# Row gathers of the third and fourth tile issued behind the first packed-query gathers

## The chip, the cores and the metric

The kernel runs on one core of a Trainium2 chip. The time is the device time of one execution in microseconds (us). The numbers for a kernel are the median, the lowest and the highest of several executions; beside them stands one execution taken with the hardware profiler, from which all durations, waits and start times in this text come. Times "at 692.27" are us from the start of the profiled span.

The engines have short names in the profile: PE multiplies matrices, PEld is its weight load, DVE is the vector engine, ACT the scalar engine, POOL the GpSimd engine, SP the engine that issues most plain DMAs. POOL issues the indirect DMAs (row gathers through a list of indices) beside its own arithmetic.

## The reference

Four graph layers run one after the other on x of 8 batches x 2048 nodes x 64 channels. Every layer normalises its input, attends over the neighbours of each node that a sparse 2048 x 2048 matrix names, and adds the result to x.

```python
# --- layer 0 (adj_preln) ---
h = jnp.maximum(_layernorm(x, axis=-1), 0.0)
x = x + _L0_gnn_ref(h, adj)
# --- layer 1 (adj_preln) ---
h = jnp.maximum(_layernorm(x, axis=-1), 0.0)
x = x + _L1_gnn_ref(h, adj, L1_gnn_W, L1_gnn_a)
# --- layer 2 (adj_preln) ---
h = jnp.maximum(_layernorm(x, axis=-1), 0.0)
x = x + _L2_gnn_ref(h, adj, L2_gnn_Wh, L2_gnn_bh, L2_gnn_Wo, L2_gnn_bo, L2_gnn_gamma, L2_gnn_beta)
# --- layer 3 (adj_preln) ---
h = jnp.maximum(_layernorm(x, axis=-1), 0.0)
x = x + _L3_gnn_ref(h, adj, L3_gnn_W, L3_gnn_a)
```

The change lies in layer 2, in its first half, which has four heads (H = 4, D = 64):

```python
def _gat_layer(h, mask, b):
    scores = jnp.einsum('...nd,...md->...nm', h, h)
    scores = jnp.where(mask, scores, NEG)
    attn = jax.nn.softmax(scores, axis=-1)
    return jnp.einsum('...nm,...md->...nd', attn, h) + b
...
h = jnp.einsum('bnc,hdc->bhnd', x, Wh)
out_h = _gat_layer(h, mask[None, None], bh[None, :, None, :])
cat = jnp.transpose(out_h, (0, 2, 1, 3)).reshape(B, N, H * D)
z = jax.nn.leaky_relu(cat, negative_slope=0.2)
h2 = jnp.einsum('bnk,dk->bnd', z, Wo)
out2 = _gat_layer(h2, mask[None], bo)
```

Since q·k of two projected nodes is x_n (Wh^T Wh) x_m, the kernel stores per node the products x_n (Wh^T Wh) of all heads once, and then scores each edge against the plain row x_m of the neighbour.

## The kernel before

**Tiles and slots.** The 2048 nodes are cut into 16 tiles of 128. In a tile, each of the 128 nodes sits on one partition. The first neighbours of each node fill whole slots: `ROWS[i]` slots of tile i hold one neighbour for every node. The further neighbours of the nodes that have more are packed: `PACKED[i]` slots of tile i hold an arbitrary edge on each partition. A slot's neighbour rows come by one indirect DMA, "a row gather", which POOL issues in `gather` (L246 to L255): 128 rows of 512 numbers of 4 bytes, 256 KB, into one of the 26 places of `ring` (`RING`, L33), a buffer that all tiles share in turn. A tile's places come free when its last user is done.

**The queries of the four heads.** At the end of layer 1 `products` (L321 to L336) makes for each tile the 2080 numbers per node (8 batches x 4 heads x 64, and 32 norms) and SP stores them in the table `qtab` (L336), 1040 KB per tile. For a `ROWS` slot the tile's own products `q` serve as they are: for the first two tiles of layer 2 they are still in SBUF (`kept`), for the others SP loads them (L741) into one of two buffers. For a packed slot each partition needs the products of another node, so POOL gathers them from `qtab` (L730, `qe`, 1040 KB each) into one of `QE` = 4 buffers. `fetch` issues those gathers in the order of use; the fifth needs the buffer of the first, which is free once DVE has subtracted the norms (L760) of the first.

**Layer 2, first half** (L714 to L850). `pipeline(take2, first2, second2, third2, fourth2)` runs the tiles in the order `ORDER2 = [8, 9, 10, 12, 11, 13, 0, ...]`, each stage one tile behind the stage ahead of it:
- `take2` issues the row gathers of the tile, the load of its own rows (L736), the load of `q` (L741) and up to four `qe` gathers.
- `first2` scores: per slot ACT copies the row to PSUM (`g2`, L753, one buffer), DVE multiplies it with `q` or `qe` (L755), sums (L759), subtracts (L760), and ACT takes the exponential (`w`, L761).
- `second2` weights: per slot and per pair of heads k POOL multiplies row and weight (`wh`, L772, three buffers) and for some tiles adds two such products (L785); PE sums them over slots in PSUM (L787), starting from the tile's own rows (L779); ACT divides (`yn`, L795).
- `third2` and `fourth2` project with PE, ACT and DVE and store the rows that the second attention reads.

Slots of the first tiles, `ROWS` + `PACKED`: tile 8 has 3 + 1, tile 9 has 3 + 1, tile 10 has 3 + 1, tile 12 has 1 + 2, tile 11 has 1 + 2, tile 13 has 2 + 1, tile 0 has 9 + 8. The first six sum to 21 slots; the ring of 26 has room for five of tile 0.

**What sets the order.** The text of the program doesn't fix the order on an engine. The Tile framework takes the instructions with their dependencies and lays out each engine's sequence itself, with a simulated timeline (`schedule_with_timeline_sim=True`). On the chip each engine then runs its sequence as laid out, and waits where a semaphore isn't there yet. In the sequence before, POOL issues around the start of layer 2's first half: 26 row gathers, four `qe` gathers, three L772 and one L785 of tile 8, a fifth `qe` gather, and then L772 of tile 8's packed slot. Each DMA of POOL signals on one of eight semaphores in turn, and waits, before it is issued, for the DMA eight before it.

Of the kernel before, what the change touches and what calls it, by code (L numbers as in the profile page):

```python
# [1 line left out]

# [32 lines left out]

PAIRS = [0, 0, 2, 2, 2, 0, 0, 0, 2, 2, 2, 2, 2, 2, 2, 2]
QE = 4


MAKING = [15, 14, 13, 0, 12, 11, 10, 1, 9, 2, 8, 3, 7, 4, 6, 5]  # L40
# [19 lines left out]
def edge_stack(ctx: ExitStack, tc: tile.TileContext, x_in, adj, w1, w1t, a1, wh, wht, bh, wo, bo,  # L60
# [9 lines left out]
    nc = tc.nc  # L70
# [141 lines left out]
    order = list(MAKING)  # L212
# [33 lines left out]
    def gather(k, i, st):  # L246

        n = SLOTS[i]
        assert sum(SLOTS[j] for j in held) + n <= RING
        held[i], front[0] = front[0], (front[0] + n) % RING  # L250
        cols = table[k].shape[1]
        for t in range(n):
            nc.gpsimd.indirect_dma_start(  # L253
                out=ring[:, (held[i] + t) % RING, :cols], out_offset=None, in_=table[k][:, :],
                in_offset=bass.IndirectOffsetOnAxis(ap=idx[:, OFF[i] + t:OFF[i] + t + 1], axis=0))  # L255

    def load(st, name, src, bufs):
        st[name] = rows_pool[0].tile([P, F], F32, name=name, bufs=bufs)
        nc.sync.dma_start(out=st[name], in_=src)

    def rows_of(k, i):
        return table[k][i * P:(i + 1) * P, :F]
# [451 lines left out]
    with tc.tile_pool(name="l2", bufs=2) as l2p, \  # L714
# [5 lines left out]
        thin[0] = ps_z  # L720

        stream = [(i, t) for i in order for t in range(PACKED[i])]
        sent = {}

        def fetch(upto):

            while len(sent) <= min(upto, len(stream) - 1):
                i, t = stream[len(sent)]
                q = sent[i, t] = l2p.tile([P, QW], F32, name="qe", bufs=QE)
                nc.gpsimd.indirect_dma_start(  # L730
                    out=q, out_offset=None, in_=qtab[:, :],
                    in_offset=bass.IndirectOffsetOnAxis(ap=qidx[:, POFF[i] + t:POFF[i] + t + 1], axis=0))

        def take2(i, st):
            gather(2, i, st)
            load(st, "rows", rows_of(2, i), 3)  # L736
            if i in order[:2]:
                st["q"] = kept[i]
            else:
                st["q"] = own_pool[0].tile([P, QW], F32, name="q")  # L740
                nc.sync.dma_start(out=st["q"], in_=qtab[i * P:(i + 1) * P, :])  # L741
            fetch(stream.index((i, 0)) + min(PACKED[i], QE) - 1)

        def score(i, st, lo, hi):

            K, n = ROWS[i], hi - lo
            w = l2p.tile([P, max(ROWS), B * H], F32, name="w2", bufs=5)[:, :n]
            st.setdefault("w", []).append(w)
            s = ps_s.tile([P, F], F32, name="s2")[:, :n * B * H].rearrange("p (t c) -> p t c", c=B * H)
            for t in range(lo, hi):  # L750
                q = st["q"] if t < K else sent[i, t - K]
                g = ps_g.tile([P, F], F32, name="g2")
                nc.scalar.copy(g, row(i, t))  # L753
                pr = l2p.tile([P, B * H, D], F32, name="prod2")
                nc.vector.tensor_tensor(  # L755
                    pr.rearrange("p (b h) d -> p b h d", h=H),
                    q[:, :B * H * D].rearrange("p (b h d) -> p b h d", h=H, d=D),
                    heads(g)[:, :, None, :].to_broadcast([P, B, H, D]), op=OP.mult)
                nc.vector.tensor_reduce(s[:, t - lo, :], pr, AX.X, OP.add)  # L759
                nc.vector.tensor_tensor(s[:, t - lo, :], s[:, t - lo, :], q[:, B * H * D:], op=OP.subtract)  # L760
                nc.scalar.activation(w[:, t - lo], s[:, t - lo], AF.Exp, bias=mbb[:, OFF[i] + t:OFF[i] + t + 1])  # L761
                if t >= K:
                    fetch(stream.index((i, t - K)) + QE)

# [66 lines left out]
        def fourth2(i, st):  # L831
# [14 lines left out]
            store_rows(3, i, h2, False)  # L846

        pipeline(take2, first2, second2, third2, fourth2)
        thin[0] = None
    own.close()  # L850
# [541 lines left out]
def whole_stack(tc, t, out):  # L1392
    nc = tc.nc
    D = t["gamma"].shape[0]
    with tc.tile_pool(name="flag", bufs=1) as pool:
        flag = pool.tile([1, 1], I32, name="flag")
        edge_stack(tc, t["x"], t["adj"], t["w1"], t["w1t"], t["a1"], t["wh"], t["wht"], t["bh"], t["wo"],
                   t["bo"], t["gamma"], t["beta"], t["w3"], t["w3t"], t["a3"], out, flag)
        bad = nc.values_load(flag, min_val=0, max_val=1)
        with tc.If(bad > 0):  # L1400
            gnn_stack(tc, t["x"].rearrange("n (b d) -> n b d", d=D), t["adj"], t["w1"], t["a1"], t["wht"],
                      t["bh"], t["wo"], t["bo"], t["gamma"], t["beta"], t["w3"], t["a3"],
                      out.rearrange("n (b d) -> n b d", d=D))
# [36 lines left out]
```

## Time and profile before

| what | value |
|---|---|
| three executions | median 1720.55 us, 1719.27 to 1725.79 us |
| the profiled execution, device time | 1721.51 us |
| its span from first to last instruction | 1719.7 us |
| mean granted PE clock in it | 0.875 |
| busy in the span: PE, DVE, POOL, ACT | 1215.1, 1318.4, 1153.4, 744.5 us |
| row gathers (L253), all layers | 405, 986 ns each on POOL |
| `qe` gathers (L730) | 32, 986 ns each on POOL |
| L772 `wh` | 162, 1918 ns each on POOL |
| L755 and L759, the two long DVE steps of one scored slot | 2276 to 2282 ns and 2286 ns |

The first half of layer 2 lies between about 660 and 1215 us of the span. In the groups of instructions, "busy" is the sum over a group, "idle before" the time in which the engine stood still just ahead of the group's members, with what ended most of it. A DMA issued by POOL shows there only the time of its issue; when its data have landed shows in who waited for it. In the timeline a bracket gives the idle time before an instruction and what ended it. "issue" means that nothing in the profile was waited for.

### The profile page before, as it was taken

The numbers are of one execution on the slowest core, as the hardware profiler recorded it, in microseconds if no ns is written. First come the engines' busy times: TensorE is split into PE (matmuls) and PEld (weight loads), VectorE is DVE, ScalarE is ACT, GpSimd is POOL, SyncE is SP. The second block draws the span as 40 slices with busy tenths as digits, with TensorE's granted clock in tenths as the row PEclk, the third lists the DMA queues.
The fourth block names the chain that finished last, engine by engine and source line by source line (L and its number), as shares of the span: only waits on it lengthen the run. The fifth ranks groups of instructions, "written<-read, shape, count | busy, mean of one in ns | idle before, by whom it ended". The sixth has DMA issues, their size and how long they took to land.

```text
span 1719.7 us, 15784 instructions
## 1 busy us (share of the span) xinstructions
PE 1215.1 (71%) x3771; PEld 606.6 (35%) x3771; DVE 1318.4 (77%) x2748; ACT 744.5 (43%) x2378; POOL 1153.4 (67%) x903
## 2 busy tenths in 40 slices
PE   0025667776479974599997999999467877555877
PEld 0002334443234431234342444443223433333545
DVE  6979999992469987699997899831389889823656
ACT  5841324441146783356531545545234445620011
POOL 5766867786554125898789889985577896654540
PEclk9998876896699997799999999999787879657989
DMA  5555454455566447656255345200643542235651
GB/s 172 167 182 179 152 200 153 141 198 156 147 201 235 158 179 260 233 189 208 87 201 200 113 157 177 87 13 19 255 141 99 154 146 70 81 119 164 197 170 51
DMA packets 85787, 266.94 MB, mean 155 GB/s; under 512 B 14627, under 2 KB 14659, under 8 KB 75446
## 3 DMA queue, kind: packets, MB, share of 16 engines
q0 software_dynamic: 37328, 141.05, 26.7%
q1 hardware_dynamic: 48358, 124.79, 20.4%
q8 instruction: 32, 0.52, 0.1%
q14 instruction: 69, 0.57, 0.1%
HBM read 208.74 MB, written 57.05 MB: 155 GB/s over the span
## 4 chain that ended last, share of the span: by engine, by line
PE 25%; POOL 11%; DVE 9%; issue 7%; ACT 5%; DMA 3%; another core or an unknown queue 2%; DVEq 0%; SPq 0%; POOLq 0%; ACTq 0%
PE y L787 10%; PE y L385 4%; POOL g L253 3%; POOL wh L772 3%; PE m L836 2%; ACT yn L795 2%; PE m L824 2%; PE y L779 2%; POOL wg L380 1%; DMA g<-table,idx 1%; POOL ln_r L290 1%; DMA rows<-table 1%; PE m L399 1%; DVE prod L755 1%
## 5 line engine op out<-in xcount | busy, mean ns | idle before, releaser
L253 POOL DMA_INDIRECT g<-table,idx x405 | 399.2, 986 | 233.5 <-issue 161.7
L772 POOL TENSOR_TENSOR wh<-g,w 128x1024 f32<-128x1024 f32 x162 | 307.5, 1918 | 30.0 <-PE y L787 28.0
L385 PE MATMUL y<-wg,ident 128*128 128x512 f32 x392 | 234.5, 729 | 72.7 <-POOL wg L380 64.3
L290 POOL TENSOR_TENSOR ln_r<-ln_q,mhalf 128x8 f32<-128x8 f32 x80 | 135.8, 1701 | 160.6 <-DVE ln_q L288 85.1
L759 DVE TENSOR_REDUCE s<-prod 128x32 f32<-128x2048 f32 x81 | 184.0, 2286 | 14.8 <-ACT w L761 12.9
L380 POOL TENSOR_TENSOR wg<-g,w 128x1024 f32<-128x1024 f32 (+1 forms) x91 | 158.9, 1756 | 37.3 <-ACT w L436 24.2
L787 PE MATMUL y<-wh,ident 128*128 128x512 f32 x320 | 154.6, 610 | 28.9 <-POOL wh L785 25.1
L385 PE MATMUL y<-wg,selt 128*128 128x512 f32 x256 | 141.6, 663 | 5.4 <-POOL wg L380 4.4
L385 PEld LDWEIGHTS y<-wg,ident 128*128 128x128 f32 x392 | 81.6, 228 | 162.2 <-POOL wg L380 78.9
L787 PE MATMUL y<-wh,selt 128*128 128x512 f32 x256 | 124.7, 614 | 10.4 <-POOL wh L772 10.4
L795 ACT ACTIVATE yn<-y,rec 128x64 f32<-128x64 f32 x512 | 111.2, 368 | 27.5 <-PE y L787 26.9
L755 DVE TENSOR_TENSOR prod<-q,g 128x2048 f32<-128x2048 f32 x49 | 111.5, 2276 | 5.3 <-ACT g L753 4.6
L399 PE MATMUL m<-w,selt 128*128 128x8 f32 (+1 forms) x384 | 59.5, 258 | 76.0 <-ACT w L542 38.2
L380 DVE TENSOR_TENSOR wg<-g,tiny 128x1024 f32<-128x1024 f32 (+1 forms) x92 | 98.2, 1086 | 17.1 <-PE y L385 8.8
L399 PEld LDWEIGHTS m<-w,selt 128*128 128x128 f32 x384 | 63.5, 213 | 122.3 <-ACT w L542 43.6
L442 DVE SCALAR_TENSOR_TENSOR zt<-m,bhc,att 128x512 f32<-128x512 f32 x64 | 47.3, 738 | 75.0 <-ACT att L441 74.4
L298 ACT ACTIVATE xh<-x,ln_r 128x64 f32<-128x64 f32 x256 | 88.3, 428 | 18.8 <-POOL ln_r L292 18.7
L787 PEld LDWEIGHTS y<-wh,ident 128*128 128x128 f32 x320 | 59.0, 193 | 104.9 <-issue 63.8
L428 PE MATMUL q<-rows,sel 128*128 128x512 f32 x128 | 84.3, 762 | 15.7 <-DVE prod L422 5.0
L753 ACT COPY g<-g 128x512 f32<-128x512 f32 x81 | 50.4, 622 | 100.5 <-DVE prod L755 87.9
L755 DVE TENSOR_TENSOR prod<-qe,g 128x2048 f32<-128x2048 f32 x32 | 73.0, 2282 | 17.0 <-DMA qe<-qtab,qidx 15.9
L779 PE MATMUL y<-rows,ident 128*128 128x512 f32 x128 | 70.0, 634 | 18.3 <-DMA rows<-table 13.6
(210 smaller groups left out, 2584.7 us busy)
## 6 DMA issues: line engine op xcount, KB each, us to landing
qtab<-q SPq DMA_DIRECT2D x16, 1040.0 KB
a<-in_adj_dram SPq DMA_DIRECT2D x16, 1024.0 KB
q<-qtab SPq DMA_DIRECT2D x14, 1040.0 KB
table<-xh SPq DMA_DIRECT2D x48, 256.0 KB
rows<-table SPq DMA_DIRECT2D x48, 256.0 KB
xs<-x SPq DMA_DIRECT2D x48, 256.0 KB
x<-xs SPq DMA_DIRECT2D x48, 256.0 KB
table<-xh SPq DMA_DIRECT2D x32, 260.0 KB
```

The lines of the kernel that those rows point to most:

```text
L253: nc.gpsimd.indirect_dma_start(out=ring[:, (held[i] + t) % RING, :cols], out_offset=None, in_=table[k][:, :], in_offset=bass.IndirectOffse ...
L290: nc.gpsimd.tensor_tensor(st["rstd"][:, 0, :], q, mhalf, op=OP.pow)
L298: nc.scalar.activation(dst[:, b * D:(b + 1) * D], st["src"][:, b * D:(b + 1) * D], func, bias=0.0 if st["less"] is None else r[:, 1, b:b + ...
L380: eng.tensor_tensor(wg[:, :m].rearrange("p t (b d) -> p t b d", b=B), g[:, :, :F].rearrange("p t (b d) -> p t b d", b=B), w[:, t0:t0 + m, ...
L385: nc.tensor.matmul(y, lhs(i, t), wg[:, t - t0, :], start=(t == 0 and own is None), stop=(t == n - 1))
L399: nc.tensor.matmul(p[:, :cols], selt(i, t), packed[:, t, :], start=(t == 0), stop=(t == T - 1))
L755: nc.vector.tensor_tensor(pr.rearrange("p (b h) d -> p b h d", h=H), q[:, :B * H * D].rearrange("p (b h d) -> p b h d", h=H, d=D), heads(g ...
L759: nc.vector.tensor_reduce(s[:, t - lo, :], pr, AX.X, OP.add)
L772: nc.gpsimd.tensor_tensor(wg, heads(row(i, t))[:, :, None, :].to_broadcast([P, B, 2, D]), w[:, :, 2 * k:2 * k + 2, None].to_broadcast([P, ...
L779: nc.tensor.matmul(st["ys"][j], ident, xb[:, 4 * j:4 * j + 4], start=True, stop=False)
L787: nc.tensor.matmul(st["ys"][j], lhs(i, t), wg[:, 4 * j:4 * j + 4], start=False, stop=(t == n - 1))
L795: nc.scalar.activation(yn[:, b, h, :], st["ys"][j][:, b, h, :], AF.Copy, scale=st["rec"][:, 4 * j + b, 2 * k + h:2 * k + h + 1])
```

## The change

In `take2` the row gathers of the tiles at places 2 and 3 of the order (the third and the fourth, tiles 10 and 12) get an edge to a `qe` gather: the one that was newest when `take2` of the tile two places ahead had ended. For tile 10 that is the `qe` gather of tile 8, for tile 12 that of tile 9. `issue_after` adds no wait on a semaphore: it tells the scheduler that each of these seven gathers has to stand behind that instruction in POOL's sequence. Nothing is added or removed; every gather moves the same bytes to the same place.

```diff
+BEHIND, LATER = 2, 4
...
-        sent = {}
+        sent, newest, lately = {}, [None], []
...
                 q = sent[i, t] = l2p.tile([P, QW], F32, name="qe", bufs=QE)
-                nc.gpsimd.indirect_dma_start(
+                newest[0] = nc.gpsimd.indirect_dma_start(
                     out=q, out_offset=None, in_=qtab[:, :],
                     in_offset=bass.IndirectOffsetOnAxis(ap=qidx[:, POFF[i] + t:POFF[i] + t + 1], axis=0))
 
         def take2(i, st):
-            gather(2, i, st)
+
+            n = order.index(i)
+            with tc.issue_after(lately[n - BEHIND].ins) if BEHIND <= n < LATER else nullcontext():
+                gather(2, i, st)
             load(st, "rows", rows_of(2, i), 3)
...
             fetch(stream.index((i, 0)) + min(PACKED[i], QE) - 1)
+            lately.append(newest[0])
```

The sequences that the scheduler lays out differ as follows. POOL, from the start of layer 2's first half, before: 26 row gathers; `qe` 1 to 4; L772 x3 and L785 of tile 8; `qe` 5; L772 of tile 8's packed slot. After: 19 row gathers; `qe` 1 to 4; 4 row gathers; L772 x3 and L785 of tile 8; `qe` 5; 3 row gathers; L772 of tile 8's packed slot. From there the two sequences hold the same instructions, with `qe` gathers shifted by one to four places among the L772, forward for the next tiles and backward within tile 0.

On ACT, up to tile 0, copies of rows and exponentials of the scores (L753, L761) stand ahead of eight-fold groups of divisions (L795) behind which they stood before, at seven places; the long DVE steps move ahead of short ones in the same way. On SP, five loads and stores move by up to two places. From the middle of tile 0's packed slots the sequences agree again for the rest of layer 2's first half.

The second half of layer 2 and layer 3's start (L859 to L902, between about 1255 and 1530 us of the span) touch nothing that the change touches, but the scheduler lays them out anew: there 330 DVE instructions, 297 of ACT, 170 of PE and 60 of POOL stand at other places than before, by at most 18, 25, 12 and 5 places. The largest moves belong to two tiles whose divisions and layer norms (L465, L881 to L883, L890) go 15 to 18 places back and forward. Layer 3's rest is as before.

More of the change, by code (lines that the diff above doesn't have):

```diff
@@ L1 @@
-from contextlib import ExitStack
+from contextlib import ExitStack, nullcontext
 import concourse.bass as bass
```

## The prediction

> **What bounds the kernel now.** I looked first at where in the span the change lies, with the busy time of each engine by stretch (columns: stretch, its length; busy time and instructions of PE, PEld, DVE, ACT, POOL; PE clock; share of the DMA engines' time; GB/s).
>
> ```profile
> 660.00:684.60 24.60, 7.20 (x12) 2.16 (x10) 22.17 (x18) 5.70 (x12) 18.66 (x20) 0.63 0.90 319
> 684.60:701.00 16.40, 0.00 (x0) 0.00 (x0) 0.52 (x2) 0.00 (x0) 13.48 (x13) 0.50 0.91 314
> 701.00:770.00 69.00, 59.28 (x154) 23.91 (x154) 67.59 (x59) 36.16 (x121) 63.57 (x39) 0.93 0.55 186
> 770.00:806.70 36.70, 35.95 (x106) 16.38 (x105) 33.97 (x33) 22.21 (x77) 34.08 (x24) 1.00 0.69 231
> 806.70:828.50 21.80, 18.82 (x58) 8.13 (x58) 20.56 (x19) 15.21 (x50) 15.91 (x10) 1.00 0.24 78
> 828.50:890.60 62.10, 59.75 (x181) 26.87 (x179) 60.63 (x47) 27.53 (x75) 46.49 (x30) 1.00 0.48 163
> 890.60:950.50 59.90, 44.48 (x102) 18.25 (x102) 47.40 (x43) 17.55 (x57) 55.65 (x40) 0.94 0.56 186
> 950.50:1100.00 149.50, 148.68 (x429) 66.75 (x430) 138.14 (x116) 78.45 (x247) 132.44 (x83) 1.00 0.45 149
> ```
>
> From 684.6 to 701 PE and ACT do nothing and DVE nearly nothing: only POOL and the DMA engines work. That hole is what the change can shorten. From 701 on three engines are almost full at once, so a shorter hole need not be a shorter program; PE is fullest from 770 to 890 and from 950 on, POOL between. Then the timeline of the hole (start, length, engine, instruction; in brackets the idle time before it and what ended it):
>
> ```profile
> 684.24 0.32 SPq L741 DMA_DIRECT2D q<-qtab  x1
> 684.25 0.29 ACT L761 ACTIVATE w<-s,mbb 128x32 f32<-128x32 f32 x1 [2.60 <-issue]
> 684.57 0.26 DVE L403 TENSOR_REDUCE row<-w 128x32 f32<-128x96 f32 x1 [0.35 <-issue]
> 684.75 0.95 POOL L253 DMA_INDIRECT g<-table,idx  x1 [0.31 <-issue]
> ...
> 691.02 0.95 POOL L253 DMA_INDIRECT g<-table,idx  x1 [0.30 <-issue]
> 692.27 0.95 POOL L730 DMA_INDIRECT qe<-qtab,qidx  x1 [0.31 <-issue]
> ...
> 696.98 5.65 POOL L772 TENSOR_TENSOR wh<-g,w 128x1024 f32<-128x1024 f32 x3
> 700.71 2.29 DVE L755 TENSOR_TENSOR prod<-qe,g 128x2048 f32<-128x2048 f32 x1 [15.88 <-DMA qe<-qtab,qidx]
> 702.58 2.34 POOL L785 TENSOR_TENSOR wh<-wh 128x1024 f32<-128x1024 f32 x1
> ...
> 704.98 6.60 PE L787 MATMUL y<-wh,ident 128*128 128x512 f32 x8 [22.20 <-POOL wh L785]
> ...
> 707.90 0.98 POOL L730 DMA_INDIRECT qe<-qtab,qidx  x1 [2.97 <-DVE s L760]
> 708.90 5.65 POOL L772 TENSOR_TENSOR wh<-g,w 128x1024 f32<-128x1024 f32 x3
> ```
>
> DVE had scored tile 8's three plain slots by 684.6 and waited 15.88 us for the first `qe`. POOL issued it only at 692.27, behind 26 row gathers at one per 1.255 us from 659.58. PE waited 22.2 us for the first L785: the weights of tile 8 were there at 684.5 (the exponential at 684.25), but POOL's multiplications stood behind the last seven row gathers and four `qe` issues. Last, could `qe` have gone earlier? SP's own waits:
>
> ```profile
> SPq L741 <- DMA qtab<-q: 3.7, 1, 3.7
> SPq L741 <- DVE s L760: 7.4, 2, 6.9
> ```
>
> The load of `q` stood behind the stores of `qtab` for 3.7 us from 673.4, so the stores were in by 677.1; the rest of its wait was for a buffer. Nothing but its place held `qe` back.
>
> **What the Trainium skill says.** (1) "Perfetto Trace Analysis", Per-instruction lifecycle, SWDGE part: the profile's interval of a DMA that GpSimd issues is the making of its descriptors, not the moving. The trace agrees: L730 takes 0.95 us and its user starts 8.4 us after its start. (2) "DMA: Bandwidth & Descriptors", Anatomy of one DMA: about 2.0 us + bytes / 436e3 for one GpSimd DMA alone. For 1,064,960 bytes that is 4.4 us (estimate); the trace has 8.4 with the engines 0.91 busy, so I use 8.4 and keep 4.4 as its lower end. (3) The same page, Queues, rings and completion order: each DMA engine takes the queues that have work in turn. So the `q` load of 1040 KB on SP's queue, issued at 684.24 in both kernels, would share with an earlier `qe`; no run here shows that yet. (4) "TensorE: Matmul & The Clock Gate", on queue depths: vector, scalar and GpSimd engines run their queues strictly in order. The trace agrees: POOL's ready multiplications waited behind issues for 12.5 us.
>
> **The change part by part**, against the profiled execution (1721.51 us, 0.96 above the median; I subtract that at the end).
>
> *First `qe`.* Seven gathers leave its front: 7 x 1.255 = 8.8 us, issue at 683.5, after 677.1 and so without a wait. It lands 8.4 us later, at 691.9; if the `q` load takes half of the engines until it is through, about 1.5 us later (until 690.7 each gets some 165 of 330 GB/s), 693.4; by the page's price 687.9. I take 692.3. DVE's lead over before: 700.7 - 692.3 = 8.4 us (6.9 to 12.8).
>
> *POOL up to tile 8's first product.* Before: 30 issues ahead of L772; after: 19 + 4 + 4 = 27. 3 x 1.255 = 3.8 us: 696.98 becomes 693.2, PE's first L787 704.98 becomes 701.2.
>
> *POOL up to tile 8's packed slot.* The three issues are not gone, they stand behind the fifth `qe`. So at L772 of 708.90 POOL has issued as much as before and gains only the wait that vanishes: 2.97 us for L760 of the first `qe`. In the new order L760 comes at 692.3 + 6.7 = 699.0 (before 700.71 and 707.43), POOL asks at 701.2: no wait. Gain 2.9 us. The three gathers of tile 12 now signal on the semaphores of `qe` 2, 3 and 4 and wait for those: in the trace before the DMA engines had moved all four `qe` and all gathers by 706, and `qe` 4 now has four gathers behind it, 1.05 MB or 3.2 us at 330 GB/s, so about 702.5; the third gather asks at 704.9. No cost; one of 2 us if I am off by 4. Tile 10's rows land by about 705; DVE needs the first after tile 9, before at 724.66, so some 716 now: hidden.
>
> *From there to tile 0.* From 708.90 to 802 POOL has only gaps of 0.16 us, same instructions in both: it stays 2.9 ahead, no more. From 770 PE follows. Between 770 and 890.6 PE is idle 0.75 + 2.98 + 2.35 = 6.1 us, and POOL waits at 883.74 and 890.42 for DVE's L760 (2.23 + 3.75). Both are stalls on DVE or on ACT behind it; DVE itself is idle under 7 us from 701 to 895. If DVE keeps its lead, PE can win back up to 6.1 more: 2.9 to 9.0. DVE's lead is bounded by ACT, which copies its rows in order with the divisions that wait for PE; the seven score pairs that move ahead of divisions let it be about one slot (2.28 + 2.29 us) ahead of PE. I take half: 2.9 + 3.1 = 6.0 us. The moved pairs cost ACT 0.59 + 0.29 us each ahead of a division, hidden while ACT is 44% to 70% busy.
>
> *Tile 0 and behind.* POOL paces 890 to 950, PE to 1215; sequences there agree, so 6.0 stays 6.0. The `qe` gathers within tile 0 move one to two L772 (1.9 us each) back; before, the first was issued at 851.18 and used at about 861.4, 10.2 us, against 5 to 8.4 for landing: nothing left over, but covered.
>
> *Second half of layer 2.* It is laid out anew. No row tells what that does; DVE is 90% busy from 1260 to 1460 and no engine is full. An instruction that DVE does 18 places later is 18 x 0.486 us = 8.7 us later (223 us in 459 instructions from 1260 to 1510); one 18 places earlier gains as much. With two tiles moved opposite ways I take 0, ends -9 and +17.
>
> Sum: 1721.5 - 6.0 = 1715.5; on the median 1714.6. I say **1715**.
>
> **Rivals.**
> - *DVE sets the pace* and its lead of 8.4 survives whole, with 1.6 more from POOL's two waits on L760. For: 67.6 of 69 us busy, and L760 ends POOL's waits. Against: POOL's gap-free 93 us, where it is only 2.9 ahead. 1721.5 - 10 = 1711.5, and 1706 with luck in the second half.
> - *The gain is hidden*: PE is held by POOL's 2.9 at first and by its yn and y buffers later, and the second half gives 2 to 3 back. For: PE 98% busy in two stretches. Against: it is PE that waits in the hole. 1720 to 1722.
> - *Slower: the new layout of the second half.* Place: the DVE steps L881 to L890 of one tile at about 1470 us, 15 to 18 places late, and the tile behind it held by the same order: 2 x 8.7 = 17.3 us. For: the moves are there, and DVE is too full to catch up. Against: other tiles' work fills the places. 1721.5 - 3 + 17 = 1735; it decides from 15 us of loss on against a gain of 6.
>
> That the change doesn't do what it says is out: the sequences show `qe` behind 19 gathers instead of 26.
>
> **How the numbers follow.** What a measurement can tell from no change is about 0.5%, 8.6 us. The likeliest case (1711 to 1719) 0.40, of which 0.16 lies past -0.5%; DVE's pace 0.30, all faster; hidden 0.12; slower layout 0.18, nearly all past +0.5%. Faster 0.16 + 0.30 + 0.01 = 0.47, same 0.24 + 0.10 + 0.01 = 0.35, slower 0.18. The range 1705 to 1729 leaves out two thirds of the last case and a little of the first rival.
>
> **What would show it.** The first `qe` issued near 683.5 and DVE's wait for it 7 to 9 us instead of 15.88; L772 starting near 693.2; no wait on L760 ahead of the fifth `qe`; tile 8's packed L772 near 706; PE idle under 3 us from 770 to 890; the last L836 of the first half 6 us before 1210.68. Wrong if the three gathers of tile 12 wait for `qe`, if DVE waits for tile 10's rows, or if the time from 1215 to the end, 504.5 us now, changes by more than 5.

## The result and the profile after

| | before | after |
|---|---|---|
| executions, side by side on one chip | 1722.52 us median (1715.06 to 1727.59, 20 runs) | 1729.74 us median (1723.97 to 1737.92, 20 runs) |
| ratio to before | | 1.0042, 95% interval 1.0027 to 1.0056 |
| profiled execution: span | 1719.7 us | 1723.8 us |
| first row gather of layer 2's first half | 659.58 | 655.55 |
| first half: from there to ScalarE's last copy (L844, now L851) | 555.7 us | 554.6 us |
| second half: from there to the store of the mean row (L366, now L369) | 311.6 us | 320.8 us |
| from there to the end | 192.8 us | 192.8 us |

The changed kernel is 7.2 us slower by the medians. Its layers 0 and 1, which the change doesn't touch, took 4.0 us less in the profiled execution, so positions below are counted from the first row gather. Lines in the changed kernel have numbers higher by 3 up to `take2` and by 7 behind it.

The hole did shrink. Busy time by stretch, after (same stretches and columns as in the prediction):

```profile
660.00:684.60 24.60, 5.60 (x6) 1.46 (x6) 19.64 (x16) 3.32 (x8) 18.51 (x21) 0.53 0.97 336
684.60:701.00 16.40, 4.46 (x7) 2.26 (x8) 13.56 (x11) 2.20 (x5) 14.48 (x11) 0.50 0.92 365
701.00:770.00 69.00, 59.66 (x165) 24.78 (x165) 62.60 (x57) 38.61 (x126) 65.11 (x41) 0.96 0.56 190
770.00:806.70 36.70, 36.51 (x107) 16.43 (x107) 31.81 (x30) 22.87 (x83) 31.57 (x22) 1.00 0.55 189
806.70:828.50 21.80, 19.60 (x56) 7.81 (x54) 21.41 (x17) 11.74 (x39) 18.41 (x12) 1.00 0.19 58
828.50:890.60 62.10, 56.42 (x168) 25.88 (x169) 60.16 (x49) 28.59 (x81) 46.60 (x30) 0.97 0.52 180
```

From 684.6 to 701 DVE is busy for 13.56 us where it was 0.52. But from 701 to 770, DVE has 62.6 us to do instead of 67.6 and PE's busy time hardly differs (59.7 and 59.3 us): DVE's early start doesn't become PE's. These stretches lie at the same times of the span, so in the changed kernel 4.0 us further on in the work; moved back by 4.0 us they give DVE 11.2 and 62.7 us and PE 59.8, which says the same. The timeline of the hole, after:

```profile
679.45 0.94 POOL L733 DMA_INDIRECT qe<-qtab,qidx  x1 [0.30 <-issue]
...
687.37 2.29 DVE L762 TENSOR_TENSOR prod<-qe,g 128x2048 f32<-128x2048 f32 x1 [4.77 <-DMA qe<-qtab,qidx]
...
689.16 5.66 POOL L779 TENSOR_TENSOR wh<-g,w 128x1024 f32<-128x1024 f32 x3
...
697.28 0.99 POOL L733 DMA_INDIRECT qe<-qtab,qidx  x1 [0.16 <-issue]
698.58 0.95 POOL L256 DMA_INDIRECT g<-table,idx  x1 [0.30 <-issue]
...
702.04 5.66 POOL L779 TENSOR_TENSOR wh<-g,w 128x1024 f32<-128x1024 f32 x3
```

`qe` is issued 8.8 us nearer to the first row gather, DVE starts on it 9.3 us nearer, POOL's first product stands 3.8 us nearer, the fifth `qe` waits for nothing, and the packed product of tile 8 is 2.8 us nearer. All five are near what the prediction worked out. The time went elsewhere. The two halves of layer 2 as one stretch each, before and then after:

```profile
659.58:1215.32 555.74, 480.70 (x1353) 208.17 (x1351) 431.72 (x377) 264.87 (x839) 459.08 (x293) 0.95 0.43 146
1215.32:1526.89 311.57, 205.48 (x580) 106.80 (x580) 249.23 (x508) 143.78 (x470) 226.97 (x175) 0.76 0.41 135
```

```profile
655.55:1210.12 554.57, 483.07 (x1355) 209.70 (x1354) 433.19 (x378) 266.34 (x841) 459.11 (x293) 0.95 0.43 146
1210.12:1530.96 320.84, 212.88 (x580) 108.71 (x580) 255.20 (x508) 144.28 (x469) 227.09 (x175) 0.74 0.40 132
```

The first half is 1.2 us shorter, not 6.0. The second half, which computes exactly what it did, is 9.3 us longer; the same 508 DVE instructions are busy 6.0 us longer in it, and DVE stands idle 3.3 us longer. -1.2 + 9.3 = +8.1 us, beside 7.2 us by the medians.

### The profile page after: what moved, and what is told of

The parts are those of the page before. It is cut to its first block, busy times and chain, and to the rows that moved or that the text cites. A ratio compares the mean times of both kernels' runs of the same rounds, so it can differ in the third digit from the quotient of the medians.

```text
span 1723.8 us, 15789 instructions
## 1 busy us (share of the span) xinstructions
PE 1224.4 (71%) x3771; PEld 611.7 (35%) x3771; DVE 1325.3 (77%) x2748; ACT 745.5 (43%) x2378; POOL 1152.1 (67%) x903
## 5 line engine op out<-in xcount | busy, mean ns | idle before, releaser
L293 POOL TENSOR_TENSOR ln_r<-ln_q,mhalf 128x8 f32<-128x8 f32 x80 | 135.9, 1702 | 159.0 <-DVE ln_q L291 95.9
L388 PE MATMUL y<-wg,selt 128*128 128x512 f32 x256 | 137.7, 648 | 3.5 <-POOL wg L383 3.2
L310 ACT COPY xt<-q 128x512 f32<-128x512 f32 x80 | 46.2, 580 | 81.9 <-PE q L309 63.0
```

Source lines behind the costliest of these rows:

```text
L293: nc.gpsimd.tensor_tensor(st["rstd"][:, 0, :], q, mhalf, op=OP.pow)
L388: nc.tensor.matmul(y, lhs(i, t), wg[:, t - t0, :], start=(t == 0 and own is None), stop=(t == n - 1))
```

## The experiments

To separate the change from what the scheduler makes of it, a helper ties each engine's sequence to a given list. The program's instructions have the same names in both kernels, so the sequence of one kernel can be laid on the other; the tie (`NO_WAIT` is a dependency without synchronisation) is an edge for the scheduler alone and puts no wait into the program. B1 and B2 are the lists of the first half and of the second half (with layer 3) from the kernel before, A1 and A2 those from the changed kernel; the code cuts below name the lists instead of printing them.

```diff
+def pinned(tc, nc, orders):
+    named = {i.name: i for i in nc.cur_bb.bb.instructions}
+    for order in orders:
+        for a, b in zip(order, order[1:]):
+            tc.add_manual_dep(named[f"I-{b}"], f"I-{a}", NO_WAIT, reason="pinned")
```

All measured times, with the two halves from each profiled execution. A ratio is to the kernel before on the same chip; the f and g runs fell on chips where the kernel before takes 1673 us instead of 1723 (in f1, which has its sequences, layers 0 and 1 take 17 us less and the end 27, the halves of layer 2 are as long).

| run | median us | ratio to before, 95% interval | first half | second half |
|---|---|---|---|---|
| e1: A1 + B2 | 1721.41 | 0.9991 (0.9979 to 1.0003) | 553.8 | 315.9 |
| e2: B1 + A2 | 1732.39 | 1.0043 (1.0027 to 1.0060) | 556.0 | 320.3 |
| e3: A1, `qe` of tile 0 as in B1, + B2 | 1720.73 | 0.9980 (0.9964 to 0.9996) | 556.0 | 311.9 |
| e4: third tile held only | 1719.73 | 0.9975 (0.9961 to 0.9988) | 554.8 | 308.5 |
| e5: B1 + A2 early part | 1732.87 | 1.0048 (1.0037 to 1.0059) | 555.9 | 321.2 |
| e6: B1 + A2 late part | 1735.32 | 1.0068 (1.0041 to 1.0094) | 555.9 | 326.9 |
| e7: B1 + e4's second half | 1723.13 | 0.9993 (0.9977 to 1.0010) | 555.3 | 309.0 |
| e8: B1 + second half of LATER = 6 | 1727.02 | 1.0011 (0.9996 to 1.0026) | 556.4 | 316.7 |
| e9: A1 up to tile 0, then B1, + B2 | 1726.09 | 1.0003 (0.9992 to 1.0015) | 556.1 | 313.9 |
| e10: the move alone, + B2 | 1723.70 | 0.9986 (0.9969 to 1.0002) | 553.0 | 313.7 |
| e11: B1 + B2, extra matmuls | 1728.29 | 1.0019 (1.0003 to 1.0036) | 556.1 | 317.3 |
| e12: the move alone + e4's second half | 1718.16 | 0.9977 (0.9964 to 0.9990) | 552.4 | 315.9 |
| f1: B1 + B2, stride | 1675.08 | 1.0004 (0.9991 to 1.0016) | 555.7 | 311.8 |
| f2: B1 + A2, stride | 1679.32 | 1.0036 (1.0019 to 1.0052) | 556.2 | 317.7 |
| f3: e12, stride | 1670.29 | 0.9980 (0.9970 to 0.9991) | 552.7 | 309.1 |
| g1: B1 + B2, no scale step | 1672.87 | 0.9994 (0.9984 to 1.0005) | 555.5 | 307.1 |
| g2: B1 + A2, no scale step | 1674.68 | 1.0009 (1.0000 to 1.0018) | 555.0 | 312.3 |
| g3: e12, no scale step | 1666.54 | 0.9957 (0.9943 to 0.9971) | 552.7 | 302.0 |

One profiled execution is not a median: with the same B2, behind different first halves, the second half took 311.6, 311.9, 313.7, 313.9 and 315.9 us, and with e4's order 308.5, 309.0 and 315.9 us (e4, e7, e12).

### Which half costs the time

e1, the changed kernel with the second half held in the old order:

```diff
+        pinned(tc, nc, B2)
```

> The changed kernel, with the instructions of the second half of layer 2 and of layer 3 held on every engine in the order that they have in the kernel before; the first half keeps the order of the changed kernel. Theory (the new order of the second half costs the time): the 9.3 us that the second half took longer are gone, the 1.2 us that the first half took less remain, so 1 us below the kernel before, ratio 0.9993, and the second half (last aggregate product to the store of the mean row) again 312 us. Rival (the held gathers cost the time where they are, in their own half, or leave late buffers behind): 6 to 8 us above the kernel before, ratio 1.004.

e2, the kernel before with the second half in the new order:

```diff
+        pinned(tc, nc, A2)
```

> The kernel before, with the instructions of the second half of layer 2 and of layer 3 held on every engine in the order that they have in the changed kernel; no gather of the first half is held. Theory (order of the second half): 9 us above the kernel before, ratio 1.005, and its second half 321 us. Rival (held gathers): no difference from the kernel before, ratio 1.000.

Measured by the medians: 1.9 us below the kernel before (e1; it can't be told from none) and 9.1 us above it (e2). Both are what the theory said; only e1's second half is longer than the 312 us expected, in an execution 5.5 us above e1's median. No held gather is in e2, and it is no faster than the changed kernel. Its second half has the changed kernel's mark:

```profile
662.20:1218.15 555.95, 480.62 (x1353) 208.20 (x1351) 431.66 (x377) 264.87 (x839) 459.07 (x293) 0.96 0.43 146
1218.15:1538.45 320.30, 212.07 (x580) 108.53 (x580) 255.08 (x508) 144.03 (x469) 227.16 (x175) 0.75 0.41 132
```

So the order of work that the change doesn't touch costs the whole loss: shown.

### Which part of that order

e5 has the new order up to about 1420 us, e6 behind it:

```diff
-        pinned(tc, nc, A2)
+        pinned(tc, nc, [a[:cut[e]] + b[cut[e]:] for e, a, b in each(A2, B2)])   # e6: each(B2, A2)
```

> The kernel before, with the new order in the first two thirds of the second half alone (up to about 1420 us of the span, 152 Vector Engine instructions elsewhere, by a few places each); the rest of the second half is held in the order before. Theory A (many small moves add up: by 1400 us the kernel with only the second half new is some 7 us behind): 5 to 8 us above the kernel before, ratio 1.003 to 1.005. Rival B (the two tiles moved by 15 to 18 places, which lie after 1420 us, cost it, as my prediction's slower case had it): no difference, ratio 1.000.

> The counterpart: the order before up to about 1420 us, the new order in the last third of the second half, where the two tiles stand 15 to 18 places elsewhere on Vector Engine. Theory A (small moves early on): 1 to 4 us above the kernel before, ratio 1.001 to 1.002, the rest of the 9 us. Rival B (the two tiles): the whole 9 us, ratio 1.005.

Measured: +8.7 us and +11.1 us. Both theories fall in part. The early part costs all of it although nothing moves far there; the late part, with the two tiles that moved by 15 to 18 places, also costs all of it; together they cost no more than one alone. An order's cost isn't a sum over its moves.

Counted from the start of each second half, DVE starts its 318th instruction at 199.2 us before and 6.8 us later in e2 (206.0), so most of the changed order's loss comes in its early part. e6 doesn't show that the two tiles cost anything. It is 1.4 us late at the 318th instruction and 15.1 us late at the 346th, ahead of where those tiles' steps stand (from the 374th on, in either order), and 15.4 us late at the end. Right behind its cut, DVE waits (e6):

```profile
1422.58 0.69 DVE L301 TENSOR_REDUCE ln_q<-ln_sq 128x8 f32<-128x512 f32 x1 [6.77 <-ACT ln_sq L289]
...
1432.50 0.69 DVE L444 TENSOR_TENSOR prod<-q,g 128x512 f32<-128x512 f32 x1 [3.87 <-PE q L442]
...
1435.95 0.69 DVE L444 TENSOR_TENSOR prod<-q,g 128x512 f32<-128x512 f32 x1 [2.15 <-PE q L442]
```

In e2, where the same late part follows the new early part, no DVE wait between 175 and 275 us of the half is over 1.5 us. So e6 measures the new late part behind the old early one, a pair that the scheduler never made. What a move can look like, at the first place where the orders part (DVE, before and then e2):

```profile
1273.87 0.16 DVE L882 TENSOR_REDUCE most<-rec 128x1 f32<-128x8 f32 x1
1274.07 0.20 DVE L883 RECIPROCAL rec<-rec 128x8 f32<-128x8 f32 x1
1274.21 1.82 DVE L422 TENSOR_TENSOR prod<-q,g 128x1024 f32<-128x1024 f32 x2
1275.95 0.69 DVE L465 TENSOR_TENSOR y<-y,rec 128x512 f32<-128x512 f32 x1
```

```profile
1276.83 0.16 DVE L896 TENSOR_REDUCE most<-rec 128x1 f32<-128x8 f32 x1
1277.95 0.70 DVE L479 TENSOR_TENSOR y<-y,rec 128x512 f32<-128x512 f32 x1 [0.95 <-PE y L399]
1278.56 0.19 DVE L897 RECIPROCAL rec<-rec 128x8 f32<-128x8 f32 x1
1278.66 1.77 DVE L436 TENSOR_TENSOR prod<-q,g 128x1024 f32<-128x1024 f32 x2
```

The division of one tile (L465, L479 in e2) has moved ahead of the reciprocal and the products of the next. In its old place PE's sum was ready; in its new place DVE stands for 0.95 us with ready work queued behind. This is one such wait; the loss as a whole wasn't traced wait by wait.

### Other orders

e4 is the changed kernel with one tile less held, e7 and e8 put other kernels' second halves behind the old first half:

```diff
-BEHIND, LATER = 2, 4
+BEHIND, LATER = 2, 3
```

> The changed kernel with LATER = 3: only the third tile's row gathers are held behind the first tile's gathers of packed queries, and all that follows is ordered by the scheduler afresh (378 Vector Engine instructions of the second half stand elsewhere than in the changed kernel, 359 elsewhere than in the kernel before). Theory (the second half's length is a matter of the order that happens to come out): the first half gives 1 to 3 us, the second half lies anywhere from 9 us shorter to 17 us longer than in the kernel before, with no relation to how much is held. Rival (the held gathers cost the time in proportion): about half of the changed kernel's loss, 3.5 us above the kernel before, in the first half's neighbourhood.

```diff
+        pinned(tc, nc, E4_2)   # e8: the second half of the kernel with LATER = 6
```

> The kernel before, with the second half in the order that the kernel with only the third tile held (LATER = 3) has there. Theory (the second half's time goes with whatever order came out, nothing else): 3 to 5 us below the kernel before, ratio 0.9975, which is what that kernel gained, less 1 us for its first half. Rival (that kernel gained because it holds fewer gathers): no difference from the kernel before.

> The kernel before, with the second half in the order that comes out when four more tiles are held (LATER = 6): a third draw of that order, with 316 Vector Engine instructions elsewhere than before. Theory (orders are draws that spread by some 10 us): a time of its own between 5 us below and 12 us above the kernel before, most likely over 2 us from it either way. Rival (what matters is one particular move of the changed kernel, other new orders cost nothing): within 1.5 us of the kernel before.

Measured: e4 -3.6 us, e7 -1.1 us, e8 +2.8 us. Holding one tile less turned a loss of 7.2 into a gain, so the loss is not in proportion to what is held. e7 gained less than expected; its interval and e8's include no change at all, so e7's theory isn't confirmed. Behind the old first half, three orders of the scheduler's lie at -1.1 (e7), +2.8 (e8) and +9.1 us (e2), and the two that were pieced together from old and new at +8.7 and +11.1 us (e5, e6): the order alone moves the time by some 10 us, and the old order is one of the good ones.

### The first half

e3 puts the `qe` gathers of tile 0 and behind back to their old places; e9 goes back to the old order on every engine from tile 0's third product on; e10 is the move that the diff asks for and nothing else.

```diff
+        pinned(tc, nc, A1_with_POOL_of(B1, since="tile 0") + B2)            # e3
+        pinned(tc, nc, A1_until("tile 0, third product") + B1_since + B2)   # e9
+        pinned(tc, nc, B1_with_POOL_of(A1, until="packed L779") + B2)       # e10
```

> As the kernel with the new first half and the old second half, and GpSimd's order in the fifth tile of the first half (tile 0) and after it taken from the kernel before too, so that the gathers of packed queries there stand one to two products earlier again (17 places differ). Theory (the first half lost its lead because those gathers slipped behind products): 1.2 to 1.6 us less than without this, so 2.5 us below the kernel before, ratio 0.9985, and the last aggregate product of the first half 2.8 us nearer to the first row gather than in the kernel before. Rival (the lead was lost to Vector Engine's waits for the 16 buffers and comes to nothing whatever the order): the same time as without it, within 0.3 us in the first half.

> The changed kernel's first half up to the third scored slot of tile 0 (about 800 us), from there the order before on every engine, and the second half in the order before. What differs from the run with the whole first half new: Vector Engine no longer does tile 13's three short steps on the reciprocal, which wait 1.52 us for a product of TensorE and push the next reduction to where it waits 1.09 us for ScalarE, ahead of tile 0's third product. Theory (that place is where Vector Engine's lead, 4.5 us at 800 us, falls to under 1): the lead at that product stays 4 us or more, and the first half takes 3 to 4.5 us less than in the kernel before, ratio 0.998. Rival (GpSimd and TensorE pace tile 0, and the lead is lost anyway): first half 1 to 2 us shorter, as with the whole first half new.

> The diff's wording alone: GpSimd's gathers up to the packed product of the second half-finished tile stand as in the changed kernel (27 places), and every other instruction on every engine stands as in the kernel before, in both halves. Theory (GpSimd's 2.9 us are gained by the move itself, and ScalarE's order before, with copies behind divisions, keeps Vector Engine from running further ahead): the first product of tile 8's packed slot 2.8 us nearer to the first gather, the first half 1.5 to 3 us shorter than in the kernel before, ratio 0.9985. Rival (the gain came from the scheduler's new order of ScalarE and Vector Engine, the move alone brings nothing): first half as before within 0.5 us, ratio 1.000.

e3's and e9's theories fall, and so do their rivals, which had the first half 1 to 2 us shorter: it is 0.2 and 0.4 us longer than before. That e3 as a whole lies 2.6 us below the kernel before, as its theory said, is luck as far as the theory goes; its profile doesn't show where the 2.6 us come from. e10's theory holds in the first half: 2.8 us shorter, and POOL's lead is 2.9 us at tile 8's packed product, 2.5 us at 749 and at 830, 2.8 us at 1176 (times of the kernel before). The changed kernel keeps 2.3 us of it at 853 and 1.2 us from 903 on. Where its DVE loses its own lead (tile 0, after):

```profile
794.49 0.19 DVE L767 TENSOR_TENSOR s<-s,q 128x32 f32<-128x32 f32 x1
796.20 0.19 DVE L814 SCALAR_TENSOR_TENSOR rec<-m,row 128x32 f32<-128x32 f32 x1 [1.52 <-PE m L402]
...
798.09 2.29 DVE L766 TENSOR_REDUCE s<-prod 128x32 f32<-128x2048 f32 x1 [1.09 <-ACT w L768]
800.30 2.28 DVE L762 TENSOR_TENSOR prod<-q,g 128x2048 f32<-128x2048 f32 x1
```

A short step of the tile before stands ahead of ready work and waits. e9 takes that step away, and DVE's lead goes at the same product by another way, from 4.3 to 1.7 us and then to nothing (ScalarE and then DVE of e9):

```profile
799.52 3.38 ACT L816 ACTIVATE yn<-y,rec 128x64 f32<-128x64 f32 x16 [4.18 <-PE y L808]
802.67 0.71 ACT L774 COPY g<-g 128x512 f32<-128x512 f32 x1
```

```profile
803.41 2.29 DVE L776 TENSOR_TENSOR prod<-q,g 128x2048 f32<-128x2048 f32 x1 [3.24 <-ACT g L774]
```

ScalarE's divisions wait for PE, the copy of DVE's next row stands behind them, and DVE is pulled back to the pace of PE and, ahead of it, POOL. The same is seen in e10, whose DVE and ScalarE keep the old order: DVE's lead is 7.2 us at its first `qe` product and 1.3 us six products later, while POOL keeps 2.9. So DVE's lead over POOL brought nothing in these runs. And POOL's two waits on DVE in tile 0 stayed (2.23 and 3.75 us before), as did PE's behind them, 1.29 and 2.47 us where they were 0.86 and 1.64 (after):

```profile
878.16 0.98 POOL L733 DMA_INDIRECT qe<-qtab,qidx  x1 [2.10 <-DVE s L767]
...
884.85 0.98 POOL L733 DMA_INDIRECT qe<-qtab,qidx  x1 [3.76 <-DVE s L767]
```

### TensorE's clock

PE's granted clock in the second half is 0.76 before and 0.74 after. e11 asks whether more work for PE there raises the clock and shortens the stage:

```diff
         if own is not None:
+            nc.tensor.matmul(y[:, :F // 2], ident, own[:, :F // 2], start=True, stop=True)
             nc.tensor.matmul(y, ident, own, start=True, stop=False)
```

> The kernel before with 16 extra matmuls in the second half, one per tile, of half the width, ahead of the first product of each aggregate, which overwrites them; all else in the order before. They are 16 x about 0.8 us = 13 us of work that the result doesn't need, in a stage where TensorE stands still for 105 of 312 us. Theory (TensorE's low granted clock, which costs 46 us of its busy time there, lengthens the second half, and more work keeps it higher): the time at a low clock falls, the second half gets 2 to 6 us shorter. Rival A (TensorE's clock follows from the waits and doesn't set the time, the extra work fits in its idle time): within 2 us. Rival B (TensorE sits on the chain of waits at those places): up to 13 us longer.

```profile
L393 PE MATMUL y<-rows,ident 128*128 128x512 f32 x32 | 20.6, 733 | 0.0
L392 PE MATMUL y<-rows,ident 128*128 128x256 f32 x32 | 13.1, 500 | 24.8 <-DMA g<-table,idx 14.0 <-DVE z L461 10.8
```

The extra work (L392) is 13.1 us busy; the kernel takes 3.0 us more by the median (0.5 to 6.2 by its ratio). More work didn't make the stage shorter, so the theory falls. But the clock in the second half stayed at 0.76, so e11 doesn't test what a higher clock would bring; nor does it decide between the rivals. The other profiles do tell that the 0.02 isn't what the new order costs: e5 has 0.76, as before, and takes 321.2 us, while e10 and f1 have 0.73 and 0.74 with the old order and take 313.7 and 311.8 us.

### By what the second half gets longer

The 6.0 us that DVE is busy longer in the changed kernel sit in one row of its groups: the norm's scale step, second half, before and then after.

```profile
L288 DVE TENSOR_SCALAR ln_q<-ln_q 128x8 f32<-128x8 f32 x32 | 12.2, 383 | 0.2
```

```profile
L291 DVE TENSOR_SCALAR ln_q<-ln_q 128x8 f32<-128x8 f32 x32 | 18.6, 583 | 0.2
```

The longest of the 32 after, in the timeline of all engines:

```profile
1423.26 3.98 DVE L291 TENSOR_SCALAR ln_q<-ln_q 128x8 f32<-128x8 f32 x1
1423.42 3.77 POOL L383 TENSOR_TENSOR wg<-g,w 128x1024 f32<-128x1024 f32 x2
1427.32 1.67 POOL L293 TENSOR_TENSOR ln_r<-ln_q,mhalf 128x8 f32<-128x8 f32 x1
1429.02 0.59 ACT L301 ACTIVATE xh<-ln_xc,ln_r 128x64 f32<-128x64 f32 x2 [5.25 <-POOL ln_r L293]
```

Two thirds of these steps take under 0.3 us. This one takes 3.98 us and ends 0.05 us after the second of two POOL products; the five longest of each kernel all end 0.02 to 0.05 us after an arithmetic step of POOL. The Trainium skill, "SBUF — State Buffer", section "SBUF: two separate sides", says that vector engine and GpSimd share one pair of ports as an exclusive lock: where a vector step needs the pair (in a mode that uses two ports, or with two inputs in SBUF against a GpSimd step that reads SBUF), whichever of the two starts first holds it for a whole instruction, and the other is blocked. The trace agrees in that the long steps end with a POOL step. It differs in that this step starts 0.16 us ahead of POOL's first product in the profile and yet stands behind both. POOL's own next step (L293) needs the result and stands behind the products, and ScalarE waits 5.25 us for that. So the place of the step against POOL's products matters, and no dependency shows it. That was theory C: the new order costs time because this step waits longer.

The other second halves speak against it as the measure of an order (us, from the profiled executions):

| second half | length | DVE busy | of it the scale step | DVE idle |
|---|---|---|---|---|
| before, B2 | 311.6 | 249.2 | 12.2 | 62.3 |
| e2, A2 | 320.3 | 255.1 | 18.7 | 65.2 |
| e5, A2 then B2 | 321.2 | 251.8 | 15.8 | 69.4 |
| e6, B2 then A2 | 326.9 | 251.2 | 13.7 | 75.7 |
| e7, e4's order | 309.0 | 255.7 | 18.6 | 53.3 |
| e8, order of LATER = 6 | 316.7 | 252.1 | 15.2 | 64.6 |

e7 has e2's long steps and is the shortest; e6 has hardly more of them than the kernel before and is the longest. Over these orders the length follows DVE's idle time more than the step.

f1 to f3 tried to free the step by a stride, in every norm:

```diff
-        q = small.tile([P, B], F32, name="ln_q")
+        q = small.tile([P, B, 2], F32, name="ln_q")[:, :, 0]
```

> The kernel before in its own order on every engine, with the sum of squares of each norm (ln_q) laid out with a stride of two, so that its scale step on Vector Engine may no longer need the port that it shares with GpSimd. Theory C (the step waits for GpSimd's products on that port): its mean falls from 0.30 to about 0.17 us, the 12.3 us of the second half to 5.5, and the kernel gets 3 to 8 us faster, ratio 0.996 to 0.998. Rival (the step's length comes from something else, or a stride doesn't free it): its mean stays at 0.3 us and the time within 0.1%.

> The kernel before with the second half in the changed kernel's order, and the same stride of two. Theory C (the new order costs 9 us mostly because the scale step waits longer on GpSimd, 18.7 against 12.3 us): within 4 us of the run with the stride and the old order. Rival (the stall is a side effect, the order's cost lies in many small waits): still 7 to 10 us above the run with the stride and the old order.

> GpSimd's move alone in the first half, the second half in the order that came out with only the third tile held (where the scale step takes 18.8 us in sum), and the stride of two. If the stride frees the step: 5 to 12 us below the kernel before, ratio 0.993 to 0.997; if not: 4 us below, ratio 0.9977, as without it.

The stride freed nothing: the step's mean over the kernel is 305 ns in f1 and 391 ns in f2, where it was 301 before and 382 after. So f1's rival holds, and these are repetitions of e2 and e12: the new order costs 5.6 us here by the means of f2 and f1 (95% interval 3.7 to 7.6), beside 9.1 us on e2's chip (4.7 to 10.3 by its ratio).

g1 to g3 exchange the step for a reduction over one element, in the second half alone; the scale goes into ScalarE's squares, and the addition of `EPS` is left out:

```diff
-        nc.vector.tensor_scalar(q, q, INV_D, EPS, op0=OP.mult, op1=OP.add)
+        nc.vector.tensor_reduce(q, q[:, :, None], AX.X, OP.add)
...
-            nc.scalar.activation(st["sq"], st["src"], AF.Square)
+            nc.scalar.activation(st["sq"], st["src"], AF.Square, scale=INV_D ** 0.5)
```

> The kernel before in its own order on every engine; in the second half the norm's scale step on Vector Engine is exchanged for a sum over a single element, and ScalarE's squares carry the factor 1/64 (their scale is 1/8). The addition of EPS = 0.00001 is left out there. Theory C (the step waits for GpSimd on a shared port, and this wait sets the time): the exchanged step takes 0.15 to 0.2 us each time, some 6 us of sum instead of 12.3, and the kernel gets 3 to 7 us faster, ratio 0.996 to 0.998. Rival (the wait goes, but another one takes its place): ratio 0.999 to 1.000.

> The same exchange (EPS left out in the second half) with the second half in the changed kernel's order. Theory C (the longer wait, 6.4 us more, carries most of the 9 us): within 4 us of the run with the exchange in the old order, so ratio to it at most 1.0025. Rival (many small waits): 7 us or more above it, ratio 1.004 or more.

> The same exchange (EPS left out in the second half) with GpSimd's move alone in the first half and the second half in the order of the kernel that holds the third tile only, where the step took 18.8 us in sum. If the wait sets the time: 8 to 14 us below the kernel before, ratio 0.992 to 0.995. If not: 3 to 5 us below, ratio 0.997 to 0.998, as without the exchange.

The step in g2, second half:

```profile
L304 DVE TENSOR_REDUCE ln_q<-ln_q 128x8 f32<-128x8 f32 x32 | 4.9, 153 | 0.2
```

The step's 18.6 us of the changed kernel have become 4.9. In the old order that brings 1.0 us by the medians, which can't be told from none (g1: its theory falls, its rival holds). In the new order it brings more: g2 lies 2.1 us above g1 by the means (0.5 to 3.7), against 5.6 (3.7 to 7.6) with the step, a difference of 3.5 us (1.0 to 6.0). g2's theory forecast that. g3 lies 7.4 us below the kernel before where the same order with the step (f3) lay 3.1 below, less than forecast for the case that the wait sets the time (8 to 14) and more than for the other (3 to 5).

The profiled executions agree only in part. The new order's second half is 5.9 us longer with the step (f2 less f1) and 5.2 us longer without it (g2 less g1). With the step, DVE is busy 6.8 us longer and idle 0.8 us less; without it, busy 0.3 us less and idle 5.6 us longer, so most of the wait came back as other waits. That the step's wait carries a part of the changed order's cost is likely from the means; how large a part, and what the rest is, stays open.

### Both orders that came out well

e12 puts the move alone and e4's second half together:

```diff
+        pinned(tc, nc, B1_with_POOL_of(A1, until="packed L779") + E4_2)
```

> The two orders put together that each came out below the kernel before: GpSimd's move alone in the first half (all else there in the order before), and the second half in the order that came out with only the third tile held. Theory (the two halves' times add, an order's time stays with the order): 2.8 us from the first half and 1 to 3 us from the second, 4 to 6 us below the kernel before, ratio 0.997, faster than both kernels. Rival (the second half's order depends on how the first half ends, so its time comes out anew): first half 2.8 us shorter, second half anywhere from 5 us shorter to 10 us longer than 312 us.

Measured: 4.6 us below the kernel before by the medians, ratio 0.9977, and 0.9980 on another chip (f3): faster than both kernels, as expected from the sum. The profiles show the sum in f3 (552.7 and 309.1 us); e12's profiled execution, 7.7 us above its median, has the shorter first half alone (552.4 and 315.9).

## Why the prediction was wrong

The prediction said 1715 us and a gain of 6; measured were 1729.74 and a loss of 7.2. Of the signs that it named for being wrong one came: from the end of the first half to the end of the span, 504.5 us became 513.7.

- *First `qe`: right.* Issued behind 19 gathers without a wait, 8.8 us nearer; first used 7.9 us after its issue (8.4 taken), so the `q` load, issued 2.6 us behind it, cost it nothing that shows; DVE's lead 9.3 us (8.4 taken). DVE's wait was 4.77 us (7 to 9 taken), as DVE also came to it 1.8 us later.
- *POOL up to the first product and up to the packed one: right.* 3.8 and 2.8 us (3.8 and 2.9 taken); no wait on the fifth `qe`, none of the three gathers of tile 12 waits for a `qe`, DVE doesn't wait for tile 10's rows.
- *"If DVE keeps its lead, PE can win back up to 6.1 more ... I take half": this term of 3.1 us was mis-sized, it is 0.* With the move alone the first half gains 2.8 us, POOL's lead and no more (e10). DVE's lead goes where ScalarE's divisions wait for PE. PE's idle time from 770 to 890 didn't fall under 3 us, it is about 8 (0.2 + 2.2 + 5.7; 7.1 with the stretches moved back by 4.0 us).
- *"Sequences there agree, so 6.0 stays 6.0": wrong by a size.* Of POOL's 2.9 us the changed kernel keeps 1.2 (2.0 in e1, with the same sequences), since the scheduler's new places up to tile 0 give 0.8 to 1.6 back (e1's and the changed kernel's first half less e10's). Which of those places it is was tried with e3 and e9 and not found: undoing a part of them gained nothing.
- *"Second half of layer 2 ... With two tiles moved opposite ways I take 0, ends -9 and +17": this is the step that failed.* It measured +9.3 us in the profile and +9.1 us alone (e2). The zero took moves to the back and to the front as equal, each worth its places times 0.486 us. The ends of -9 and +17 took in what came; the middle had no reason behind it. The runs show no such price: in e2 DVE stands still for an operand with ready work behind it (0.95 us at the first move), and the same moves cost more or less by what stands around them (the early and the late part cost as much singly, in e5 and e6, as together in e2). Which of the new waits make up the 9 us isn't known beyond the share that the scale step may have.
- *The slower rival* had the right half of the kernel and the right sign, not the right mechanism. It put 17 us on the steps of one tile that stand 15 to 18 places late at about 1470 us. In e2 most of the loss is there before 1424 us, and the early part alone, where nothing moves far, costs 8.7 us (e5).

## What to carry to other kernels

When a scheduler lays out the program, an edge in one stage can be a new draw for a later stage that it doesn't touch: price the draw (here -1 to +9 us for three of them), not the move. Hold the other stages in their old order while you measure a local change, and look at the scheduler's orders as something to be chosen by measurement. A lead is worth only what the engine that paces the stage keeps of it, and an engine that runs its sequence in order and serves two others can hand the slower one's pace to the faster, as ScalarE did here.

## What the runs showed of the hardware

- A vector engine step of 128x8 that scales a tile in SBUF took from 0.14 to 3.98 us (changed kernel), and the five longest of each kernel's second half ended within 0.05 us of the end of a GpSimd step. A stride of two in its operand changed nothing (305 against 301 ns mean); a reduction of the same size in its place took 0.11 to 0.16 us each time (g1 and g2, second half).
- The second half with the same sequences, behind different first halves, took 311.6 to 315.9 us in five profiled executions and 308.5 to 315.9 us in three with another order, so a stage's length in one profile can't tell a difference of some 4 to 7 us.
- Chips differ by 3% in this program (1673 and 1723 us) and not in the first half of layer 2 (555.7 us in f1 as before).
- A lower granted PE clock in a stage need not mean a longer stage: 0.73 and 313.7 us (e10), 0.76 and 321.2 us (e5).
